# Unit norms behind the next product, the last unit in parts, a rotating third place and statistics by batch in a four-layer convolution kernel

## The chip, the cores and the metric

The kernel runs on one core of one Trainium2 chip, in float32. A core has a matrix engine (TensorE, PE in the profile; its weight loads are PEld), a vector engine (VectorE, DVE), an engine for activation functions (ScalarE, ACT), a general engine (GpSimd, POOL) and one that only starts transfers (SyncE, SP). They run side by side and wait for one another through semaphores. Data come from and go to HBM by DMA; SyncE, ScalarE and GpSimd can start a transfer. The metric is the device time of one execution in microseconds (us), lower is better.

## The reference, cut to what matters

The input x has shape (4, 384, 64, 64). Four layers follow, each of the form `x = x + layer(group_norm(x))`. Layer 0 is an attention block, layer 1 a filter in 8 by 8 Fourier patches with a depthwise convolution, layer 3 a 7 by 7 depthwise convolution with weights made from the data. The change lies in layer 2:

```python
y3 = bn(dw(x, c3_w, 1));  y5 = bn(dw(x, c5_w, 2))        # depthwise 3x3 and 5x5
y1 = x * c1_w + c1_b
tok = bn(kw[:, 0:1] * y3 + kw[:, 1:2] * y5 + y1)
gp = tok.mean(axis=(2, 3));  gh = gelu(bn(pw(gp, cg_w1)))
gates = sigmoid(bn(pw(gh, cg_w2)));  tok = tok * gates
h1 = gelu(bn(pw(tok, cm_w1)))                            # 384 -> 768
h2 = bn(pw(h1, cm_w2))                                   # 768 -> 384
out = gate * (tok + h2) + (1 - gate) * x
```

Each `bn` takes its mean and variance of a channel over all four batches and all positions, so all of a channel's results must exist before the next step can use any.

## The kernel before

**Stages.** Phase A does layers 0 and 1 (0 to 2567 us in the profile). Phase B does the depthwise convolutions of layer 2 and forms tok (2567 to about 3207). Phase EF is the MLP: E multiplies tok by cm_w1 (3207 to 3719), F applies the norm and Gelu and multiplies by cm_w2 (3726 to 4223). Phase G finishes layer 2 and does layer 3 (to the end). The program is written with a tile framework: the code names tiles, buffers and operations, and the framework sets waits and an order on each engine, which follows the order of the code unless an earlier operation isn't ready by its own reckoning; every engine and every DMA queue then runs its list strictly in that order.

**Phase B.** The 384 channels are cut into 12 units of 32. A unit's tile has 128 partitions, which are 4 batches by 32 channels. For a unit u, `unit_strips(u)` loads x1 (tag "x", six buffers, two for each unit), normalises it on ScalarE and, from unit 4 on, transposes it on TensorE (`strip_m`) into the strips tile z; the copies out of PSUM are at L1066 (VectorE) and L1068 (ScalarE). Then 16 steps n follow. In each, `matrices53` builds a band matrix (`toep`, L1114), `conv53` convolves two channels with both kernels (`conv_m`, L1133), ScalarE copies the result (`d_o`, L1142) and VectorE takes its statistics (`st`, L1145); after every fourth step eight channels go to HBM as `d` (L1148). After step 15 `conv_norms(u, st)` makes the scale and shift of the unit's two norms: `cn_rep` (L1164) averages the means, `cn_m` (L1173) sums over batches, a logarithm and an exponential on ScalarE give the inverse root (L312, L313), and L1183 to L1186 end with `s` and `s0`, called cn_s in the trace.

`unit_tok(u)` turns a unit into tok: it loads d back in another layout (`c_d`, L1198), adds x scaled on ScalarE (L1206), 3 by 3 (L1209) and 5 by 5 (L1211) on VectorE, squares on ScalarE (L1216) and writes tok (L1219). It is a generator of eight pieces that run between the convolutions of the next unit: in step n the loop takes a piece of tok for even n and a piece of the next unit's strips for odd n. The last unit has no next one: its eight pieces run after everything, and then `tok_stats` takes the statistics of tok (L1227 and on).

**Phase EF.** E goes through 4 batches b by 4 blocks i of 1024 positions. A tile of tok has three parts of 128 channels: two lie in the tile `e_tok` (two buffers), the third in a part of the strips tile z, at `i % 3 * 1024` (loads at L1342, scaling at L1343). h_s (L1358) is the product, e_h its copy, h_st its statistics (L1367). After the last block six aggregates over all 32 entries of h_st give h_mv (L1385), and `bn_scale_shift` (L312 to L324) the scale and shift for Gelu. F does the same for h2: it takes aggregates by batch (L1426), because the mean by batch is wanted anyway, and over all (L1429).

`over_batches` gives mean and variance over batches from those of each batch; it is used once, for tok ("ar").

Of the kernel before, what the change touches and what calls it, by code (L numbers as in the profile page):

```python
# [21 lines left out]
F32 = mybir.dt.float32  # L22
AF = mybir.ActivationFunctionType
ALU = mybir.AluOpType
AX = mybir.AxisListType
# [201 lines left out]
class _Builder:  # L227
# [99 lines left out]
    def over_batches(self, name, mv):  # L327

        nc = self.nc
        st = self.sm([P, NJ, 6], f"{name}_st")  # L330
        m = self.sm([P, NJ, 2], f"{name}_m")
        for j in range(NJ):
            nc.vector.bn_stats(st[:, j, :], mv[:, j, :, 0])
            nc.vector.bn_aggr(m[:, j, :], st[:, j, :])
        within = self.sm([P, NJ], f"{name}_w")
        nc.vector.tensor_reduce(within, mv[:, :, :, 1], AX.X, ALU.add)
        var = self.sm([P, NJ], f"{name}_v")
        nc.vector.scalar_tensor_tensor(var, within, 1.0 / B, m[:, :, 1], ALU.mult, ALU.add)
        return m[:, :, 0], var

    def bn_of_four(self, name, z, g, b, func, out):

# [620 lines left out]
    def phase_b(self):  # L963

        tc, nc = self.tc, self.nc
        with ExitStack() as ctx:
            self.open_psum(ctx, 2)  # L970
            cp = ctx.enter_context(tc.tile_pool(name="b_const", bufs=1))
            self.bx_p = ctx.enter_context(tc.tile_pool(name="b_x", bufs=6))
            self.bt_p = ctx.enter_context(tc.tile_pool(name="b_t", bufs=2))
            self.bc_p = ctx.enter_context(tc.tile_pool(name="b_c", bufs=3))
            self.band7 = self.const(cp, "band7")
            self.band7_p = self.psum.tile([P, 512], F32, tag="band", name="band7_p", bufs=1)[:, 0:W]
            nc.vector.tensor_copy(self.band7_p, self.band7)
            self.mean128 = cp.tile([P, P], F32, tag="mean128", name="mean128")
            nc.gpsimd.memset(self.mean128, 1.0 / P)
            self.taps53(0)  # L980
            self.toep = {}
            for n in range(4):
                self.matrices53(n)
            for q in range(4):
                x = self.bx_p.tile([P, 2048], F32, tag="x", name="in_x1")[:, 0:1024]
                self.strips5(0, B - 1, x, 8 * q, self.pm)
            self.units(cp)
            self.unit_x = [[] for _ in range(UNITS)]
            for u in range(UNITS):
                st = self.bt_p.tile([P, 2, 16, 6], F32, tag="st", name="st")  # L990
                strips = self.unit_strips(u + 1) if u + 1 < UNITS else iter(())
                tok = self.unit_tok(u - 1) if u else self.unit_strips(0)
                nets = iter(()) if u else self.nets(cp)
                for n in range(16):
                    if u or n > 1:
                        self.matrices53(16 * u + n + 2)
                    self.conv53(u, n, st)
                    next(strips if n % 2 else tok, None)
                    if n % 3 == 2:
                        next(nets, None)  # L1000
                self.conv_norms(u, st)
            for _ in self.unit_tok(UNITS - 1):
                pass
            self.tok_stats()
# [148 lines left out]
    def conv_norms(self, u, st):  # L1153
# [13 lines left out]
        nc.vector.scalar_tensor_tensor(d, parts[:, :, 2], 1.0 / P, d, ALU.mult, ALU.add)  # L1167

        nc.vector.tensor_copy(four[:, 1], spread(d))
        m = self.pm("cn_m")  # L1170
        for k in range(2):
            for v in range(2):
# [12 lines left out]
        nc.vector.scalar_tensor_tensor(s0, m[:, 6:7], -1.0, self.base[:, u : u + 1], ALU.mult, ALU.add)  # L1185
        nc.vector.scalar_tensor_tensor(s0, m[:, 7:8], -1.0, s0, ALU.mult, ALU.add)  # L1186
        self.tok_s = s, s0

    def unit_tok(self, u):

        nc = self.nc
        j, q = u // 4, u % 4
        s, s0 = self.tok_s
        for i in range(4):
            sl = slice(i * 1024, (i + 1) * 1024)
            d5, d3 = (self.bc_p.tile([P, 1024], F32, tag=k, name=f"c_{k}") for k in ("d5", "d3"))
            for v, d in enumerate((d5, d3)):
                nc.sync.dma_start(  # L1198
                    d.rearrange("p (y n) -> p y n", n=P),
                    self.d53[v][u][8 * i : 8 * i + 8].rearrange("y b c n -> (b c) y n"),  # L1200
                )
            for h in range(2):
                part = slice(h * 512, (h + 1) * 512)
                last = u == UNITS - 1
                m = self.psum.tile([P, 512], F32, tag="c" if last else "t", name="tok_m", bufs=4 if last else 1)
                nc.scalar.activation(  # L1206
                    m, self.unit_x[u][i // 2][:, i % 2 * 1024 + h * 512 :][:, 0:512], AF.Identity, bias=s0, scale=self.vec("c1_w")[:, u : u + 1]
                )
                nc.vector.scalar_tensor_tensor(m, d3[:, part], s[:, 1:2], m, ALU.mult, ALU.add)  # L1209
# [72 lines left out]
    def phase_ef(self, strips):  # L1282
        tc, nc = self.tc, self.nc
        with ExitStack() as ctx:
# [45 lines left out]


            st = ep.tile([P, 6, B * 8, 6], F32, tag="h_st", name="h_st")
            sums = cp.tile([P, NJ, B, 4], F32, tag="wx_sum", name="wx_sum")
            for b in range(B):
                for i in range(4):
                    blk = slice(i * 1024, (i + 1) * 1024)
                    t01 = io.tile([P, NJ - 1, 1024], F32, tag="tok", name="e_tok")
                    at = i % 3 * 1024
                    t = [t01[:, 0], t01[:, 1], self.z_[:, at : at + 1024]]
                    for j in range(NJ):  # L1340
                        for q in range(4):
# [53 lines left out]
            for b in range(B):  # L1395
# [415 lines left out]
```

## Time and profile before

| | |
|---|---|
| time, median of three runs | 5031.06 us (5026.48 to 5037.9) |
| profiled execution | span 5034.1 us |
| TensorE busy | 4606.5 us |
| VectorE busy | 2735.1 us |
| ScalarE busy | 2119.4 us |
| phase B, 2567 to 3159 us: TensorE busy | 557.7 of 592 us |
| seam from B to E, 3159 to 3207 us: TensorE busy | 4.9 of 48 us |
| E, 3207 to 3719 us: TensorE busy | 500.4 of 512 us |

A row of the timeline has the start and the time of an instruction or of several that were merged, its engine, its line (L1133 is line 1133 of the kernel before), the operation, out<-in by the program's names, and in brackets how long the engine had been idle and what ended that. SPq is SyncE's list of transfers. A row of the waits view has who waited, for whom, the total in us, the number of waits and the longest. In the waits and timelines "xN" counts records; a float32 matmul leaves two.

### The profile page before, as it was taken

To read this page: it belongs to the slowest core of one execution; us is meant where nothing else is said; L and a number is where in the kernel's file an instruction comes from. 1 tells how busy PE (TensorE), PEld (TensorE's weight loads), DVE (VectorE), ACT (ScalarE), POOL (GpSimd) and SP (SyncE) were. 2 spreads that over 40 slices of the span, in tenths; PEclk is the share of its full clock that TensorE was granted. 3 is DMA by queue.
4 is the path that set the end of the run, shared out by engine and by line. 5 is a ranking of instruction groups with operands and counts; after the bars stand their busy time and mean duration, and the time that the engine had idled before them with its cause. 6 is when DMAs were issued, how large, how long until landed. Compare 5 with 4: busy or idle time off the path is not lost. (4 is left out here: it accounts for less than half of the span.)

```text
span 5034.1 us, 48007 instructions
## 1 busy us (share of the span) xinstructions
PE 4606.5 (92%) x17875; PEld 2617.1 (52%) x17875; DVE 2735.1 (54%) x4480; ACT 2119.4 (42%) x2819; POOL 762.6 (15%) x568
## 2 busy tenths in 40 slices
PE   5999999989999899999989999699999996569999
PEld 2433444334443344435467888344444443559999
DVE  5322456644656445565867778554521114767775
ACT  4444344453544544445345666311133334652320
POOL 1000000000000000000025555000000000135543
PEclk9999999999999999998989999799999997569999
DMA  5110211110111111112259999766664333757876
GB/s 176 61 49 29 90 56 62 57 59 32 69 63 69 42 38 63 63 57 96 93 150 285 290 292 299 257 248 245 244 238 150 150 134 136 255 181 229 235 214 193
DMA packets 344919, 723.30 MB, mean 144 GB/s; under 512 B 22011, under 2 KB 172390, under 8 KB 337766
## 3 DMA queue, kind: packets, MB, share of 16 engines
q1 hardware_dynamic: 283032, 477.56, 30.5%
q0 software_dynamic: 33152, 136.60, 7.2%
q10 hardware_dynamic: 28494, 105.99, 5.4%
q8 instruction: 144, 2.36, 0.2%
q14 instruction: 97, 0.79, 0.0%
HBM read 432.48 MB, written 287.57 MB: 143 GB/s over the span
## 5 line engine op out<-in xcount | busy, mean ns | idle before, releaser
L733 PE MATMUL av<-probs,vt 128*128 128x512 f32 x2048 | 964.2, 606 | 0.0
L704 ACT ACTIVATE probs<-sc_s 128x1024 f32<-128x1024 f32 x512 | 500.1, 1021 | 758.6 <-PE av L733 743.8
L733 PEld LDWEIGHTS av<-probs,vt 128*128 128x128 f32 x2048 | 373.5, 193 | 472.0 <-issue 464.6
L924 DVE SCALAR_TENSOR_TENSOR acc<-band,vecs,acc 128x512 f32<-128x512 f32 x708 | 508.2, 747 | 43.5 <-POOL band L885 25.1
L1133 PE MATMUL conv_m<-toep,z 128*128 128x256 f32 x2304 | 519.0, 385 | 10.6 <-DVE toep L1114 6.4
L1414 PE MATMUL h_m<-f_h,cm_w_t 128*128 128x512 f32 x1152 | 496.2, 594 | 7.9 <-ACT f_h L1401 7.9
L1133 PEld LDWEIGHTS conv_m<-toep,z 128*128 128x128 f32 x2304 | 438.2, 192 | 71.6 <-DVE z L1066 4.9
L1358 PE MATMUL h_s<-e_tok,cm_w_t 128*128 128x512 f32 x768 | 364.5, 598 | 5.5 <-DVE e_tok L1343 5.5
L1414 PEld LDWEIGHTS h_m<-f_h,cm_w_t 128*128 128x128 f32 x1152 | 219.4, 191 | 284.7 <-issue 272.9
L1701 PE MATMUL conv_m<-toep,z 128*128 128x128 f32 x3072 | 367.2, 278 | 0.0
L1114 POOL TENSOR_TENSOR toep<-w,band 128x1536 f32<-128x1536 f32 x94 | 323.8, 3445 | 281.6 <-PE conv_m L1133 248.1
L1701 PEld LDWEIGHTS conv_m<-toep,z 128*128 128x128 f32 x3072 | 358.0, 195 | 0.0
L696 PE MATMUL sc_s<-q,k 32*128 32x512 f32 x2048 | 299.5, 644 | 12.6 <-ACT probs L704 10.9
L847 PE MATMUL t_m<-w_in_t,xb 128*128 128x384 f32 x768 | 278.7, 497 | 1.2 <-DVE k L622 0.6
L766 PE MATMUL proj_m<-xm,w_proj_t 128*128 128x512 f32 x576 | 268.3, 605 | 7.3 <-DVE xm L719 7.3
L1365 ACT COPY e_h<-h_s 128x1024 f32<-128x1024 f32 x96 | 97.2, 1012 | 415.5 <-PE h_s L1358 415.5
L773 DVE SCALAR_TENSOR_TENSOR x_res<-proj_m,bn_c,x_res 128x512 f32<-128x512 f32 x96 | 71.8, 748 | 339.2 <-PE proj_m L766 334.4
L1358 PEld LDWEIGHTS h_s<-e_tok,cm_w_t 128*128 128x128 f32 x768 | 147.6, 192 | 191.4 <-issue 184.6
L1422 DVE BATCH_NORM_STATS2 h_st<-f_h 128x6 f32<-128x512 f32 x72 | 49.8, 694 | 322.9 <-ACT f_h L1421 322.9
L1367 DVE BATCH_NORM_STATS2 h_st<-e_h 128x6 f32<-128x512 f32 x192 | 123.2, 685 | 185.4 <-ACT e_h L1365 185.4
L847 PEld LDWEIGHTS t_m<-w_in_t,xb 128*128 128x128 f32 x768 | 143.8, 192 | 137.1 <-issue 60.3
L1358 PE MATMUL h_s<-z,cm_w_t 128*128 128x512 f32 x384 | 196.8, 595 | 10.5 <-DVE z L1343 10.5
(369 smaller groups left out, 6298.1 us busy)
## 6 DMA issues: line engine op xcount, KB each, us to landing
d<-d_o ACTq DMA_DIRECT2D x96, 512.0 KB
c_d<-d SPq DMA_DIRECT2D x96, 512.0 KB
hid<-e_h ACTq DMA_DIRECT2D x16, 3072.0 KB
f_h<-hid SPq DMA_DIRECT2D x16, 3072.0 KB
x_in<-in_x SPq DMA_DIRECT2D x96, 256.0 KB
x_res<-in_x SPq DMA_DIRECT2D x32, 768.0 KB
xa<-x_res POOLq DMA_DIRECT2D x32, 768.0 KB, 3.7
xa_in<-xa SPq DMA_DIRECT2D x32, 768.0 KB
```

Of the source, the lines that this page charges most:

```text
L696: nc.tensor.matmul(s[:, g], lhsT=k4[32 * g : 32 * g + 32, c], rhs=q[i][32 * g : 32 * g + 32], start=True, stop=True,)
L704: nc.scalar.activation(p[:, h * 1024 : (h + 1) * 1024], s[:, 2 * h : 2 * h + 2].rearrange("p a b -> p (a b)"), AF.Exp, scale=0.25,)
L733: nc.tensor.matmul(av, lhsT=vt[:, 4 * c + v, :], rhs=p[:, v * 512 : (v + 1) * 512], start=c == 0 and v == 0, stop=c == 7 and v == 3,)
L766: nc.tensor.matmul(m, lhsT=self.w_proj[:, j, o * P : (o + 1) * P], rhs=xm[:, j], start=j == 0, stop=j == NJ - 1,)
L847: nc.tensor.matmul(m[:, 0:C], lhsT=xb[:, j], rhs=self.w_in[:, j, :], start=j == 0, stop=j == NJ - 1,)
L924: nc.vector.scalar_tensor_tensor(out, src(j, k), w, done, ALU.mult, ALU.add)
L1114: eng.tensor_tensor(t, self.w53[:, at : at + 192].rearrange("p (m n) -> p m n", n=8).unsqueeze(2).to_broadcast([P, 24, 8, 8]), band.rearra ...
L1133: nc.tensor.matmul(m[:, c * 256 : (c + 1) * 256], lhsT=self.z_[:, at : at + P], rhs=t[:, 12 * c + 4 * i : 12 * c + 4 * i + 4].rearrange("p ...
L1358: nc.tensor.matmul(s[:, v, :], lhsT=w1[:, j, o * P : (o + 1) * P], rhs=t[j][:, v * 512 : (v + 1) * 512], start=j == 0, stop=j == NJ - 1,)
L1367: nc.vector.bn_stats(st[:, o, 8 * b + 2 * i + v, :], h[:, o, v * 512 : (v + 1) * 512])
L1414: nc.tensor.matmul(m, lhsT=w2[:, o, j * P : (j + 1) * P], rhs=h[:, o, v * 512 : (v + 1) * 512], start=o == 0, stop=o == 5,)
L1701: nc.tensor.matmul(m[:, ch * P : (ch + 1) * P], lhsT=self.z_[:, at : at + P], rhs=t[:, 8 * c + 2 * i : 8 * c + 2 * i + 2].rearrange("p m a ...
```

## The change

It has four parts. First, `conv_norms` becomes a generator with two steps, and its steps run after the first and the second convolution of the next unit; a piece of the next unit's strips is now taken for even n, and a piece of tok for odd n, where the scale and shift of the unit before exist. This is to keep TensorE from standing still at the seam of two units. Second, `last_d` loads the last unit's convolution results early and in parts, into four tiles of tag "x" of 2048 columns: after the convolution of step 12 the first half of rows of the 24 channels that are already in HBM; after the loop the second half of those, then the last eight channels, some of them by GpSimd's queue. `unit_tok` of the last unit then reads these tiles. Third, the third part of tok in E goes to the place `(4 * b + i) % 3` rather than `i % 3`. Fourth, the statistics of h and h2 are aggregated for each batch and joined by `over_batches`, which is written anew for any number of columns.

```diff
     def over_batches(self, name, mv):
-        for j in range(NJ):
-            nc.vector.bn_stats(st[:, j, :], mv[:, j, :, 0])
-            nc.vector.bn_aggr(m[:, j, :], st[:, j, :])
-        within = self.sm([P, NJ], f"{name}_w")
-        nc.vector.tensor_reduce(within, mv[:, :, :, 1], AX.X, ALU.add)
-        var = self.sm([P, NJ], f"{name}_v")
-        nc.vector.scalar_tensor_tensor(var, within, 1.0 / B, m[:, :, 1], ALU.mult, ALU.add)
-        return m[:, :, 0], var
+        n = mv.shape[1]
+        mean, var = self.sm([P, n], f"{name}_m"), self.sm([P, n], f"{name}_v")
+        nc.vector.tensor_reduce(mean, mv[:, :, :, 0], AX.X, ALU.add)
+        nc.vector.tensor_scalar(mean, mean, 1.0 / B, None, ALU.mult)
+        d = self.sm([P, n, B], f"{name}_d")
+        nc.vector.tensor_sub(d, mv[:, :, :, 0], mean.unsqueeze(2).to_broadcast([P, n, B]))
+        nc.vector.tensor_mul(d, d, d)
+        nc.vector.tensor_add(d, d, mv[:, :, :, 1])
+        nc.vector.tensor_reduce(var, d, AX.X, ALU.add)
+        nc.vector.tensor_scalar(var, var, 1.0 / B, None, ALU.mult)
+        return mean, var
...
+            norms = iter(())
...
                     self.conv53(u, n, st)
-                    next(strips if n % 2 else tok, None)
+                    next(norms, None)
+                    next(tok if n % 2 else strips, None)
                     if n % 3 == 2:
                         next(nets, None)
-                self.conv_norms(u, st)
+                    if u == UNITS - 1 and n == 12:
+                        self.last_d(0)
+                norms = self.conv_norms(u, st)
+            self.last_d(1)
+            for _ in norms:
+                pass
             for _ in self.unit_tok(UNITS - 1):
                 pass
...
         nc.vector.tensor_copy(four[:, 1], spread(d))
+        yield
         m = self.pm("cn_m")
...
         self.tok_s = s, s0
+        yield
+
+    def last_d(self, step):
+        nc = self.nc
+        if step == 0:
+            self.d_last = {}
+        for h in range(2):
+            if step == h:
+                for v in range(2):
+                    self.d_last[h, v] = self.bx_p.tile([P, 2048], F32, tag="x", name="d_last")
+        parts = [(0, 0)] if step == 0 else [(1, 0), (0, 1), (1, 1)]
+        for h, late in parts:
+            c = slice(24, 32) if late else slice(0, 24)
+            for v in range(2):
+                for b in range(B):
+                    (nc.gpsimd if h and late else nc.sync).dma_start(
+                        self.d_last[h, v][32 * b + c.start : 32 * b + c.stop].rearrange("p (y n) -> p y n", n=P),
+                        self.d53[v][UNITS - 1][16 * h : 16 * h + 16, b, c].rearrange("y c n -> c y n"),
+                    )
...
+            if u == UNITS - 1:
+                d5, d3 = (self.d_last[i // 2, v][:, i % 2 * 1024 :][:, 0:1024] for v in range(2))
+            else:
...
+            hmv = ep.tile([P, 6, B, 2], F32, tag="h_mv", name="h_mv")
...
-                    at = i % 3 * 1024
+                    at = (4 * b + i) % 3 * 1024
...
-            mv = self.sm([P, 6, 2], "h_mv")
-            for o in range(6):
-                nc.vector.bn_aggr(mv[:, o, :], st[:, o].rearrange("p a b -> p (a b)"))
-            a1, c1 = self.bn_scale_shift("bn_h", mv[:, :, 0], mv[:, :, 1], self.vec("cm_g1"), self.vec("cm_b1"))
+                for o in range(6):
+                    nc.vector.bn_aggr(hmv[:, o, b], st[:, o, 8 * b : 8 * b + 8].rearrange("p a b -> p (a b)"))
+            a1, c1 = self.bn_scale_shift("bn_h", *self.over_batches("h", hmv), self.vec("cm_g1"), self.vec("cm_b1"))
...
-            mv = self.sm([P, NJ, 2], "h2_mv")
-            for j in range(NJ):
-                nc.vector.bn_aggr(mv[:, j, :], st2[:, j].rearrange("p a b -> p (a b)"))
-            a2, c2 = self.bn_scale_shift("bn_h2", mv[:, :, 0], mv[:, :, 1], self.vec("cm_g2"), self.vec("cm_b2"))
+            a2, c2 = self.bn_scale_shift("bn_h2", *self.over_batches("h2", mvb), self.vec("cm_g2"), self.vec("cm_b2"))
```

More of the change, by code (lines that the diff above doesn't have):

```diff
@@ L329, in over_batches @@
         nc = self.nc
-        st = self.sm([P, NJ, 6], f"{name}_st")
-        m = self.sm([P, NJ, 2], f"{name}_m")
-        for j in range(NJ):
-            nc.vector.bn_stats(st[:, j, :], mv[:, j, :, 0])
-            nc.vector.bn_aggr(m[:, j, :], st[:, j, :])
-        within = self.sm([P, NJ], f"{name}_w")
-        nc.vector.tensor_reduce(within, mv[:, :, :, 1], AX.X, ALU.add)
-        var = self.sm([P, NJ], f"{name}_v")
-        nc.vector.scalar_tensor_tensor(var, within, 1.0 / B, m[:, :, 1], ALU.mult, ALU.add)
-        return m[:, :, 0], var
+        n = mv.shape[1]
[9 more added lines that the diff above has]
+        return mean, var
     def bn_of_four(self, name, z, g, b, func, out):
@@ L1195, in unit_tok @@
             sl = slice(i * 1024, (i + 1) * 1024)
[L1196 to L1201, printed above, removed]
+            if u == UNITS - 1:
+                d5, d3 = (self.d_last[i // 2, v][:, i % 2 * 1024 :][:, 0:1024] for v in range(2))
+            else:
+                d5, d3 = (self.bc_p.tile([P, 1024], F32, tag=k, name=f"c_{k}") for k in ("d5", "d3"))
+                for v, d in enumerate((d5, d3)):
+                    nc.sync.dma_start(
+                        d.rearrange("p (y n) -> p y n", n=P),
+                        self.d53[v][u][8 * i : 8 * i + 8].rearrange("y b c n -> (b c) y n"),
+                    )
             for h in range(2):
```

## The prediction

> **What bounds the kernel now.** I read the page first (the 40 slices and the busy times), then sums by stage (the windows view), then the waits of TensorE and the timeline around each place that the diff touches. One page line sets the frame:
>
> ```profile
> PE 4606.5 (92%) x17875; PEld 2617.1 (52%) x17875; DVE 2735.1 (54%) x4480; ACT 2119.4 (42%) x2819; POOL 762.6 (15%) x568
> ```
>
> TensorE is busy for 92% of the span, so time can only come from its pauses. The windows view says where some lie (columns: window, its length, then busy us of PE, PEld, DVE, ACT, POOL, granted clock, DMA share, GB/s):
>
> ```profile
> 2871.00:2919.00 48.00, 46.59 (x234) 40.76 (x234) 38.38 (x74) 30.69 (x48) 27.38 (x9) 1.00 0.99 295
> 3159.00:3207.00 48.00, 4.91 (x22) 4.15 (x22) 20.00 (x76) 27.01 (x40) 0.00 (x0) 0.50 0.91 280
> 3207.00:3719.00 512.00, 500.39 (x1152) 220.38 (x1152) 258.56 (x390) 96.77 (x96) 11.47 (x16) 0.99 0.64 238
> ```
>
> The first row is one of the twelve units of phase B: TensorE rests 1.4 of 48 us, but the DMA share is 0.99. The second is the seam from B to the first MLP product, where TensorE does almost nothing for 48 us. The third is that product, 512 us with some 12 us of rest. The seam between two units, in the timeline:
>
> ```profile
> 2868.92 1.15 PE L1061 MATMUL strip_m<-ident,unit_x 128*128 128x128 f32 x8 [0.24 <-ACT z L1068]
> 2870.56 1.05 DVE L1066 COPY z<-strip_m 128x512 f32<-128x512 f32 x1
> 2870.79 0.42 PE L1164 MATMUL cn_rep<-st,mean 128*128 128x64 f32 x2 [0.72 <-DVE st L1145]
> 2871.67 1.99 PE L1133 MATMUL conv_m<-toep,z 128*128 128x256 f32 x8 [0.45 <-DVE z L1066]
> ```
>
> The norms' first product (cn_rep) stands on TensorE ahead of the next unit's first convolution and waits for the statistics of the last one; then the convolution waits for the copy of the last strip. The end of phase B:
>
> ```profile
> 3161.41 10.95 SPq L1198 DMA_DIRECT2D c_d<-d  x6
> 3163.63 0.16 DVE L1186 SCALAR_TENSOR_TENSOR cn_s<-cn_m,cn_s 128x1 f32<-128x1 f32 x1
> 3172.70 1.41 DVE L1209 SCALAR_TENSOR_TENSOR tok_m<-c_d,cn_s,tok_m 128x512 f32<-128x512 f32 x2 [8.91 <-DMA c_d<-d]
> 3187.39 0.25 DVE L1227 TENSOR_REDUCE tok_mv<-tok_sum 128x12 f32<-128x96 f32 x1
> ```
>
> The scale and shift are ready at 3163.8, but the convolution results of the last unit come back from HBM only at 3172.7. And the MLP product at the turn from batch 0 to batch 1, first in the waits of TensorE, then VectorE's and then TensorE's timeline:
>
> ```profile
> PE h_s L1358 <- DVE z L1343: 10.5, 3, 4.2
> ```
>
> ```profile
> 3338.83 0.81 DVE L1343 TENSOR_SCALAR z<-z,at,ct 128x1024 f32<-128x1024 f32 x1 [3.64 <-DMA z<-tok]
> ```
>
> ```profile
> 3339.70 1.56 PE L1358 MATMUL h_s<-z,cm_w_t 128*128 128x512 f32 x2 [3.44 <-DVE z L1343]
> 3341.05 3.19 PE L1358 MATMUL h_s<-e_tok,cm_w_t 128*128 128x512 f32 x4
> ```
>
> Three waits, one at each turn of the batch: the third place of tok goes 0, 1, 2, 0 and then 0 again, so the load has to wait for the tile before. The four matmuls after it take 3.19 us, where four take 1.7 elsewhere.
>
> [...] matmul records start 0.43 us apart in this product and 0.85 apart, four times, after the first two waits (3.4 and 4.2 us); after the third (2.9 us) none is slow. [...] the trace has 1.28 us, twice in each unit's norms (logarithm, exponential), so from cn_m to the shift takes some 5 us whatever the order.
>
> **Part 1, norms behind the next product; strips one convolution earlier.** In units 5 to 10 the cn_rep products start 48.2 us apart. The pauses at each seam (0.24, 0.72, 0.45 us and some short ones; 48.0 less 46.6 busy) are 1.4 us. After the change the next unit's first convolution (12 records of 0.214 us, 2.6 us) stands before cn_rep, and the statistics need about 1.85 us after the last convolution (the wait of cn_rep at 2619.70); the last strip is copied one convolution earlier. Both waits should be covered: 7 seams by 1.4 = 9.8, and 1.7 for a stretch at half clock after one of them (unit 8 takes 49.9 us). The first four seams are worse. Start to start on TensorE, less normal spacing: 1.65 + 2.6 and 2.1 of half clock (seam at 2619.7), 3.35 + 1.3 (2674.0), 1.65 + 1.35 (2719.3), 1.6 + 1.7 (2772.7): 17.3. But here ScalarE and the DMAs are behind for other reasons (a pause of 3.4 us before a convolution at 2696.9 that has nothing to do with norms), so I count a little over half, 9.5. Sum 21; lower end 5 (see the rivals), upper 28.8. New waits: tok's pieces and the scale and shift come one convolution later. Behind them on ScalarE and VectorE stand the copies and statistics of the next convolutions, which have four PSUM buffers, some 10 us of slack, so I charge nothing.
>
> **Part 2, last unit in parts.** The bytes stay (4 MB), the eight loads become 32. Eight go out at n = 12, under the last three convolutions (DMA share 0.86 there), eight more without the last eight channels when the slot of the unit before is free, at about 3157. The last channels are written at 3157.65 and seen as landed at 3161.4. Their first eight loads then cost 8 x 0.41 us of issue on SyncE (mean of c_d<-d) = 3.3, so 3164.7 at the earliest, and 3166 with the transfer. By bandwidth: 1.05 MB of writes, 1.57 MB and 0.52 MB of loads from 3157.65 at 280 GB/s end at 3168.9. I take 3168; the upper end is 3172.7, no gain. The shift may be 2.5 us late, since tok's last piece of unit 10 now comes after the last convolution: 3166, still earlier. From there VectorE needs four pieces of 2.66 us (3172.70 to 3175.36) = 10.7, so 3178.7 in place of 3187.4: 8.6; I take 8 (0 to 11). The chain behind it, to the first MLP matmul at 3207.4, is serial work of VectorE, ScalarE and TensorE and moves with it.
>
> **Part 3, the third place rotates.** (4b + i) % 3 never gives the same place to two tiles in a row; a place is now free two tiles (of 31 us) ahead. Removed: 10.5 us of waits and twice four matmuls at 0.43 extra = 3.4: 14. What could take its place is the load of the other two thirds (e_tok, two buffers), but at the other turns of i, where these alone bind, TensorE does not wait. 12 to 15.
>
> **Part 4, statistics by batch.** over_batches becomes seven dependent small VectorE operations; such ones start 0.2 us apart (3187.67, 3187.88, 3188.09), so 1.4 us. For ar the logarithm starts at 3192.32, after a table load that hides the old chain; the new one ends at 3192.65: +0.35. For h the last aggregate of 192 elements (1.02) becomes one of 48 (0.29 to the next start) plus 1.4: +0.7. For h2 0.96 becomes 1.4: +0.45. Together +1.5 on the path (0.5 to 2.5). The 24 aggregates by batch (0.37 each, 8.9 us instead of 6.1) lie in a stage where VectorE is busy for 259 of 512 us: nothing.
>
> **Sum.** 21 + 8 + 14 - 1.5 = 41.5; 5031.1 - 41.5 = 4989.6, say 4990.
>
> **Rivals.**
> A, the DMAs become the bound of phase B. For it: share 0.97 to 0.99 in units 4 to 10 at 292 GB/s. Against it: these units last 48.20 to 48.21 us each, with the same pauses at the same places, so TensorE's order sets them; and the first MLP product moves 315 GB/s in one stretch (3240 to 3300). If so, part 1 gives only 5, part 2 4: 5 + 4 + 14 - 1.5 = 21.5, time 5009.5.
> B, the tail gives nothing: the last write waits for the early loads of the same tensor, or 24 issues on one queue cost what they save. Time 4998.
> C, slower: tok's later turn frees the input slots later, loads of the next strips come 2.6 us late in each unit[...]: 11 x 4.3 = 47 lost, tail 0, 14 won, 1.5 lost: 5031 + 34.5 = 5065.5. Against it: six input buffers for three units.
>
> **How the numbers follow.** Chances: forecast 0.58, A 0.24, B 0.11, C 0.07. Range: all upper ends of the parts (28.8 + 11 + 15 - 0.5 = 54.3) give 4977, and A with another 3 us lost gives 5013; I put 4975 to 5013, which leaves out C and some of the tails. Faster by over 0.2% (below 5021): the first three cases less a small share, 0.88; same 0.05; slower 0.07.
>
> **What would show it.** Right: units 5 to 10 take 46.8 us with no wait at cn_rep; VectorE's first piece of the last unit starts near 3168 less what was gained before; no TensorE wait for z in the first product, which takes 497 us; the aggregate chains longer by half a us each. Wrong: units still at 48.2 us with waits on DMA (A), the write d<-d_o late (B), waits of strips or of ScalarE for x (C).

## The result, and the profile after

The changed kernel takes 5084.59 us (median of four runs, 5080.53 to 5093.9); the kernel before took 5034.48 beside it (5026.48 to 5045.41). The ratio is 1.0101, with a 95% interval of 1.0076 to 1.0125: slower by 1%, where 4990 us was forecast. The profiled execution is 47.3 us longer (span 5081.4), and the page says that TensorE works only 7.9 us more of it (4606.5 us busy before), so the rest are pauses:

```profile
PE 4614.4 (91%) x17875; PEld 2623.6 (52%) x17875; DVE 2733.3 (54%) x4508; ACT 2120.9 (42%) x2819; POOL 767.0 (15%) x576
```

The table cuts the profiled executions at events of the trace: B is from the first to the last copy `d_o` of a convolution, the seam from there to the first `h_s` matmul, E from the first to the last `h_s`, each from start to start. What lies before B (2560 to 2574 us) and after F (798 to 807) scatters by these amounts over all runs, without a change of code there, so that the three stages tell more than a single time.

| us | before | after | difference | predicted |
|---|---|---|---|---|
| B | 586.2 | 619.4 | +33.2 | -21 (part 1) |
| seam | 50.4 | 76.5 | +26.1 | -8 (part 2), +0.35 (part 4) |
| E | 510.3 | 496.9 | -13.4 | -14 (part 3) |
| last h_s to first product of F | 8.48 | 9.32 | +0.84 | +0.7 (part 4) |
| last product of F to the next | 7.66 | 8.21 | +0.55 | +0.45 (part 4) |

So parts 3 and 4 did what was worked out, and parts 1 and 2 did the opposite. The windows view of the changed kernel has the same three stretches as were shown before (window, length, busy us of PE, PEld, DVE, ACT, POOL, granted clock, DMA share, GB/s): a unit of phase B, the seam, and E.

```profile
2884.52:2935.78 51.26, 46.52 (x237) 40.66 (x235) 37.69 (x71) 29.92 (x48) 27.47 (x8) 1.00 0.86 268
3187.00:3263.00 76.00, 5.29 (x24) 4.46 (x24) 24.21 (x83) 28.83 (x43) 4.82 (x8) 0.52 0.83 188
3263.00:3760.00 497.00, 496.62 (x1151) 219.85 (x1152) 258.99 (x405) 96.19 (x95) 11.54 (x16) 0.99 0.65 242
```

In the unit TensorE now rests 4.7 us in place of 1.4, yet the DMA share has fallen from 0.99 to 0.86: the transfers aren't the bound, they are asked for too late. In E the rest is gone (0.4 of 497 us).

**Phase B.** The waits view of units 4 to 10 of the changed kernel, for TensorE, VectorE and GpSimd (total us, times, longest):

```profile
PE conv_m L1142 <- DVE z L1075: 25.4, 7, 5.2
...
DVE tok_m L1243 <- DMA c_d<-d: 38.9, 7, 6.9
...
POOL toep L1123 <- DMA w<-in_c_t: 55.7, 8, 8.4
```

The same view of the kernel before has, for its units 4 to 10:

```profile
PE conv_m L1133 <- DVE z L1066: 3.2, 7, 0.5
...
DVE tok_m L1209 <- DMA c_d<-d: 4.9, 5, 2.0
```

The wait for `cn_rep` that the change was to remove is in fact gone, and unit 1 falls from 46.7 to 42.2 us. But the convolution at each seam now waits for the strip copy `z`: 25.4 us where it was 3.2 before. In the same units VectorE waits 38.9 us for `c_d`, before 4.9. Nearly all of the loss lies in these units: from the first copy of unit 4 to that of unit 11 it is 371.3 us in place of 339.2, while units 1 to 3 together take as long as before. How the two hang together shows at one seam, first in SyncE's list and then on VectorE and TensorE (timeline of the changed kernel):

```profile
2908.23 0.34 SPq L1253 DMA_DIRECT2D tok<-c_d  x1
2908.62 1.65 SPq L1056 DMA_DIRECT2D unit_x<-x  x2
2916.53 0.34 SPq L1253 DMA_DIRECT2D tok<-c_d  x1
2916.98 1.44 SPq L1232 DMA_DIRECT2D c_d<-d  x2
2918.53 1.40 SPq L1109 DMA_DIRECT2D w<-in_c_t  x1
2920.35 3.71 SPq L1232 DMA_DIRECT2D c_d<-d  x2
```

```profile
2924.20 0.76 DVE L1243 SCALAR_TENSOR_TENSOR tok_m<-c_d,cn_s,tok_m 128x512 f32<-128x512 f32 x1 [4.45 <-DMA c_d<-d]
...
2925.97 1.04 PE L1070 MATMUL strip_m<-ident,unit_x 128*128 128x128 f32 x8
...
2931.69 1.07 DVE L1075 COPY z<-strip_m 128x512 f32<-128x512 f32 x1
...
2932.91 2.83 PE L1142 MATMUL conv_m<-toep,z 128*128 128x256 f32 x12 [3.74 <-DVE z L1075]
```

SyncE issues two loads of x, then stands 6.3 us before a write of tok that waits for VectorE's piece. Only then, at 2916.98, does it reach the loads of `c_d` and `w` for the next pieces. VectorE runs its own list in order as well: it stands 4.45 us before the tok piece, and the copy of the strip, whose transposes are done at 2927.0, comes up at 2931.69. TensorE waits for that copy. A late load has become a late convolution by way of a piece of work that TensorE itself doesn't need.

The kernel before has loads of `c_d` behind a waiting write of tok as well (SyncE's list, then VectorE):

```profile
2909.08 0.34 SPq L1219 DMA_DIRECT2D tok<-c_d  x1
2909.51 1.48 SPq L1198 DMA_DIRECT2D c_d<-d  x2
```

```profile
2919.65 0.76 DVE L1209 SCALAR_TENSOR_TENSOR tok_m<-c_d,cn_s,tok_m 128x512 f32<-128x512 f32 x1
```

There the piece that reads them comes 10.1 us after their issue and doesn't wait. In the changed kernel VectorE is ready for its piece at 2919.75, 2.8 us after the issue.

**The tail.** SyncE's list and VectorE's first piece of the last unit, in the changed kernel's timeline:

```profile
3181.96 13.26 SPq L1215 DMA_DIRECT2D d_last<-d  x7
3195.32 0.37 SPq L1253 DMA_DIRECT2D tok<-c_d  x1
3206.35 17.09 SPq L1215 DMA_DIRECT2D d_last<-d  x16
...
3232.11 1.41 DVE L1243 SCALAR_TENSOR_TENSOR tok_m<-d_last,cn_s,tok_m 128x512 f32<-128x512 f32 x2 [34.42 <-DMA e_tok<-tok]
```

The last copy of a convolution ends phase B at 3186.9; the first piece starts 45 us later, before it was 15.7 (3157.0 to 3172.70). The row names a load of `e_tok`, which came last by the records; what the piece reads is `d_last`. The last sixteen loads start one every 1.07 us (17.09 / 16), where 0.41 had been counted; 7.0 us of this are recorded as waits, 3.8 for another weight and 3.2 for earlier ones of these loads. Before the sixteen, SyncE stands for another reason (its waits view, 3176 to 3240):

```profile
SPq L1215 <- DMA cm_w_t<-in_cm_w_t: 10.6, 1, 10.6
```

This is the transfer of a weight that ScalarE has issued at 3195.09.

**E and the statistics.** In E only the wait at its start is left among TensorE's waits, and the logarithm of "ar" waits 0.31 us for the new chain (waits and timeline of the changed kernel):

```profile
PE h_s L1393 <- DVE e_tok L1378: 5.7, 1, 5.7
```

```profile
3247.87 0.17 DVE L339 TENSOR_SCALAR ar_v<-ar_v 128x3 f32<-128x3 f32 x1
3248.07 0.30 ACT L312 ACTIVATE bn_ar_a<-ar_v,eps 128x3 f32<-128x3 f32 x1 [0.31 <-DVE ar_v L339]
```

### The profile page after: what moved, and what is told of

It reads as the page before. It is cut to its first block, busy times and chain, and to the rows that moved or that the text cites. A ratio compares the mean times of both kernels' runs of the same rounds, so it can differ in the third digit from the quotient of the medians.

```text
span 5081.4 us, 48036 instructions
## 1 busy us (share of the span) xinstructions
PE 4614.4 (91%) x17875; PEld 2623.6 (52%) x17875; DVE 2733.3 (54%) x4508; ACT 2120.9 (42%) x2819; POOL 767.0 (15%) x576
## 5 line engine op out<-in xcount | busy, mean ns | idle before, releaser
L1142 PE MATMUL conv_m<-toep,z 128*128 128x256 f32 x2304 | 533.7, 391 | 35.8 <-DVE z L1075 29.1
L1448 PE MATMUL h_m<-f_h,cm_w_t 128*128 128x512 f32 x1152 | 497.0, 594 | 8.7 <-ACT f_h L1435 8.7
L697 PE MATMUL sc_s<-q,k 32*128 32x512 f32 x2048 | 298.9, 643 | 13.4 <-ACT probs L705 10.9
```

Source lines behind the costliest of these rows:

```text
L697: nc.tensor.matmul(s[:, g], lhsT=k4[32 * g : 32 * g + 32, c], rhs=q[i][32 * g : 32 * g + 32], start=True, stop=True,)
L1142: nc.tensor.matmul(m[:, c * 256 : (c + 1) * 256], lhsT=self.z_[:, at : at + P], rhs=t[:, 12 * c + 4 * i : 12 * c + 4 * i + 4].rearrange("p ...
L1448: nc.tensor.matmul(m, lhsT=w2[:, o, j * P : (j + 1) * P], rhs=h[:, o, v * 512 : (v + 1) * 512], start=o == 0, stop=o == 5,)
```

## The experiments

All are edits of the kernel before, each beside runs of it on the same chip. The stages are those of the table above.

| run | time, us | ratio to before (95%) | B | seam | E |
|---|---|---|---|---|---|
| rotation alone | 5008.07 | 0.9954 (0.9937 to 0.9971) | 587.4 | 50.0 | 495.9 |
| loop alone (part 1) | 5068.63 | 1.0083 (1.0056 to 1.0110) | 623.3 | 51.1 | 512.3 |
| last unit in parts alone (part 2) | 5058.97 | 1.0055 (1.0038 to 1.0073) | 586.3 | 76.4 | 511.6 |
| turns swapped alone | 5060.40 | 1.0047 (1.0030 to 1.0063) | 613.3 | 51.7 | 513.3 |
| norms deferred alone | 5031.74 | 0.9988 (0.9978 to 0.9998) | 578.9 | 52.9 | 514.5 |
| loop, tok written by GpSimd | 5027.34 | 0.9988 (0.9978 to 0.9998) | 575.8 | 52.3 | 512.1 |
| last loads cut by batch | 5054.32 | 1.0035 (1.0025 to 1.0046) | 587.9 | 66.9 | 514.7 |
| last loads cut by rows | 5038.35 | 1.0007 (0.9997 to 1.0017) | 586.0 | 50.7 | 512.6 |
| in parts, a weight on another queue | 5058.56 | 1.0040 (1.0025 to 1.0054) | 585.8 | 74.5 | 513.7 |
| four whole loads | 5036.00 | 1.0004 (0.9995 to 1.0013) | 585.7 | 50.3 | 509.1 |
| 16 loads by batch | 5041.85 | 1.0014 (1.0003 to 1.0024) | 586.2 | 57.3 | 513.8 |
| 16 loads by rows | 5033.76 | 0.9999 (0.9989 to 1.0009) | 587.6 | 48.6 | 511.4 |
| first combination | 5016.31 | 0.9966 (0.9954 to 0.9978) | 575.5 | 57.2 | 495.8 |
| second combination | 5011.77 | 0.9955 (0.9941 to 0.9969) | 576.5 | 51.0 | 497.0 |

### Each part alone

```diff
-                    at = i % 3 * 1024
+                    at = (4 * b + i) % 3 * 1024
```

> The kernel before with part 3 alone. Theory: the rotating place removes the three z waits and the half clock behind two of them, and nothing else moves: 13 to 15 us faster than before (5020 if before is 5034), no wait of TensorE for z in the first MLP product, which takes 497 us from first to last start. Rival: the gain only appeared in the changed kernel because its other stages moved: 0 to 5 us.

E falls by 14.4 us, to 495.9. (The half clock shows in the kernel before as a granted clock of 0.50 from 3340.30 to 3343.70 and from 3470.00 to 3473.40, behind the waits of 3.4 and 4.2 us; behind the third, from 3597.90 to 3601.30, it is 1.00.) Part 3 holds alone as in the whole: E is 495.8 to 497.0 in the four kernels with the rotation and 509.1 to 514.7 in the others. The time fell by more, 26.7 us; most of the rest lies before B and after F (9.7 and 6.3 us in the profiled executions), where no code differs.

The loop alone is part 1 as in the change (`conv_norms` in two steps, and):

```diff
-                    next(strips if n % 2 else tok, None)
+                    next(norms, None)
+                    next(tok if n % 2 else strips, None)
```

> The kernel before with part 1 alone (norms in two steps behind the next products, tok and strips swapped between even and odd steps); loads of the last unit, third place and statistics as before. Theory: the loss inside phase B is made here: units 4 to 10 take 50 to 55 us instead of 48.2, phase B's convolutions end some 30 us later, and the run is 25 to 35 us slower than before. Rival: the early loads of the last unit or the changed SBUF use cause it; then this run is within 10 us of before or faster.

B grows by 37.1 us and nothing else moves: the loss in phase B is part 1's own.

The last unit in parts alone is `last_d` of the change, with `last_d(0)` after step 12 and `last_d(1)` after the last norms:

```diff
+                    if u == UNITS - 1 and n == 12:
+                        self.last_d(0)
                 self.conv_norms(u, st)
+            self.last_d(1)
```

> The kernel before with part 2 alone (the last unit's results in 32 loads). Theory: the tail loss is made here by the number and shape of the loads: the time from the last convolution to the first MLP product grows from 50.4 to 70 to 80 us, units are as before, run 20 to 30 us slower. Rival: the tail only suffers because part 1 leaves a backlog of transfers and of tok pieces; then this run is as before or up to 9 us faster.

The seam is 76.4 us without anything of part 1: the second loss is part 2's own. The three differences by ratio, -0.46, +0.83 and +0.55%, add up to 0.92% of the whole's 1.01%. Part 4 was not run alone; what is said of it comes from the changed kernel's trace.

### What in the loop costs: the swap of turns, not the deferred norms

The swap alone, the norms left where they were:

```diff
-                    next(strips if n % 2 else tok, None)
+                    next(tok if n % 2 else strips, None)
```

> The kernel before with only the swap: tok's pieces in odd steps, strips in even ones; conv_norms stays where it was. Theory: the order in SyncE's list follows from the swap (both writes of tok stand ahead of the next loads), so this alone makes most of part 1's loss: 15 to 35 us slower, with waits of VectorE for c_d and of GpSimd for w. Rival: the later norms make the loss; then this is within 8 us of before.

B is 613.3, which is 27.1 us of the loop's 37.1, and units 4 to 10 show the signature of the changed kernel (waits view of this run):

```profile
PE conv_m L1133 <- DVE z L1066: 21.4, 7, 3.9
...
DVE tok_m L1209 <- DMA c_d<-d: 29.6, 14, 5.0
```

The deferral alone keeps the strips on odd steps:

```diff
-                    next(strips if n % 2 else tok, None)
+                    next(norms, None)
+                    if n % 2 or (u and n == 0):
+                        next(strips if n % 2 else iter(()), None)
+                    else:
+                        next(tok, None)
+                    if u and n == 15:
+                        next(tok, None)
...
-                self.conv_norms(u, st)
+                norms = self.conv_norms(u, st)
```

> The norms alone are put behind the next unit's products, in two steps; the strips keep their odd convolutions and tok's pieces the even ones (from the third on, the eighth after the last). Theory 1 (it is the swap of turns that costs, through the order of SyncE's list; the deferred norms are harmless): phase B is not longer than before, 575 to 588 us, time 5020 to 5036. Theory 2 (the deferral itself costs, because the scale and shift and so all of tok's pieces come later): phase B 600 us or more, time 5048 or more.

B falls to 578.9: theory 1. So the deferral alone is harmless and pays a little, in units 2 and 3 (49.2 to 43.3 and 54.6 to 49.6 us). On top of the swap it costs another 10 us (613.3 to 623.3); why was not followed up. But units 4 to 10 mostly stay at 48.2, and the timeline of TensorE shows why:

```profile
2896.60 1.15 PE L1070 MATMUL strip_m<-ident,unit_x 128*128 128x128 f32 x8 [0.24 <-ACT z L1077]
2898.46 0.43 PE L1173 MATMUL cn_rep<-st,mean 128*128 128x64 f32 x2 [0.72 <-DVE st L1154]
2899.34 5.45 PE L1142 MATMUL conv_m<-toep,z 128*128 128x256 f32 x24 [0.46 <-DVE z L1075]
```

Although the code has the norms after the first convolution, the framework's list has `cn_rep` ahead of it, presumably because the convolution has to wait for the last strip. The 0.72, 0.24 and 0.46 us of the kernel before are all still there. In units 4 to 10 of the kernels with the swap and tok's writes on SyncE (turns swapped, loop alone, the whole change) no wait at `cn_rep` is recorded; the longer wait for `z` stands in its place.

### Why the swap costs: loads behind writes in one list

This is the loop alone, with one line more changed in `unit_tok`:

```diff
-            nc.sync.dma_start(self.tok[u, :, :, sl].rearrange("b c n -> (b c) n"), d5)
+            nc.gpsimd.dma_start(self.tok[u, :, :, sl].rearrange("b c n -> (b c) n"), d5)
```

> The loop of the change alone (norms deferred, turns swapped), with the writes of tok issued by GpSimd in place of SyncE. Theory 1 (the loads of c_d and w stand in SyncE's list behind writes of tok that wait for VectorE): the waits of VectorE for c_d and of GpSimd for w fall to a few us in all, phase B falls from 623 to 586 or less, time 5035 or less. Theory 2 (the loads are late for another reason[...]): phase B stays at 610 to 625, time 5060 to 5070. A write on GpSimd that waits for VectorE could hold up GpSimd's own products (toep): then PE's waits for toep grow.

B falls from 623.3 to 575.8 us by the queue of one transfer alone. In units 4 to 10 (waits view of this run):

```profile
PE cn_rep L1168 <- DVE st L1149: 7.1, 5, 2.3
PE conv_m L1137 <- DVE z L1070: 6.0, 7, 1.8
...
DVE tok_m L1215 <- DMA c_d<-d: 2.9, 2, 1.8
...
POOL tok L1225 <- DVE c_d L1217: 30.9, 13, 4.6
```

The write's wait for VectorE has moved to GpSimd's list, where it holds up nothing that TensorE waits for (no wait for `toep` shows), and the waits for `c_d` are nearly gone. Over five kernels the waits of units 4 to 10 line up with B:

| us | DVE for c_d | PE for z | GpSimd for w | B |
|---|---|---|---|---|
| loop alone | 32.9 | 24.8 | 53.4 | 623.3 |
| turns swapped | 29.6 | 21.4 | 72.8 | 613.3 |
| before | 4.9 | 3.2 | 1.8 | 586.2 |
| norms deferred | 0 | 3.0 | 69.2 | 578.9 |
| loop, tok by GpSimd | 2.9 | 6.0 | 0 | 575.8 |

GpSimd's wait for `w` doesn't go with B (69.2 us where B is short): it is the late `c_d`, through VectorE's list, that costs. Nor is it SyncE's standing as such: before writes of tok it stands some 130 us in units 4 to 10 of the kernel before, 180 in the changed one, and in the run with the norms deferred (its waits view)

```profile
SPq L1230 <- DVE c_d L1222: 167.8, 28, 8.1
```

though no `c_d` is late there. The standing costs where the loads behind the write are needed soon after it, as in the seam above. That the swap brings this about is shown by the run with the turns swapped; how it moves VectorE's pieces closer to the writes was not worked out.

### Why the last unit's loads are slow

With the parts alone, SyncE's rows at the tail are

```profile
3145.20 9.26 SPq L1207 DMA_DIRECT2D d_last<-d  x8
3160.55 0.35 SPq L1245 DMA_DIRECT2D tok<-c_d  x1
3161.01 26.29 SPq L1207 DMA_DIRECT2D d_last<-d  x16
```

and SyncE was recorded as waiting 8.5 us for the transfer of a weight. To the parts alone, this run adds that the transfer of one weight, `cm_w2_t`, is given to another queue:

```diff
-            w2 = self.weight(cp, "cm_w2_t")
+            w2 = cp.tile(list(self.ins["cm_w2_t"].shape), F32, tag="cm_w2_t", name="cm_w2_t")
+            nc.gpsimd.dma_start(w2, self.ins["cm_w2_t"])
```

> The last unit's results in parts, alone (seam 76.4 us, time 5059), with the load of the weights cm_w2_t, which fell into the same stretch on ScalarE's queue, issued by GpSimd. Theory 1 (the first part loads wait 8 to 10 us[...]): the seam shortens by 8 to 10, to 66 to 68, time 5050. Theory 2 (the wait only hides the transfer, which is slow in itself): seam within 3 us of 76.

The seam is 74.5 in place of 76.4, and the last 16 loads take as long as before (26.31 us of issue):

```profile
3166.00 26.31 SPq L1207 DMA_DIRECT2D d_last<-d  x16
```

But the run doesn't decide between the theories (the loads wait for a weight, or are slow in themselves), because the edit moved the wrong weight. The views leave numbers out of names, and two weights are called `cm_w_t`. The one that SyncE waits for is `cm_w1_t`; ScalarE still issues it here, and the wait is as long as it was (ScalarE's timeline and SyncE's waits of this run):

```profile
3165.58 0.34 ACTq L282 DMA_DIRECT2D cm_w_t<-in_cm_w_t  x1
```

```profile
SPq L1207 <- DMA cm_w_t<-in_cm_w_t: 8.6, 1, 8.6
```

The one that was moved goes out only at 3215.42, after all of the loads. So no run tests whether the weight holds up the loads, and the 8.5 us (10.6 in the changed kernel) stay open. Next, number against width: the kernel before, with each of the last unit's loads in `unit_tok` replaced, at the same place, by

```diff
+                    for b in range(B):
+                        nc.sync.dma_start(
+                            d[32 * b : 32 * b + 32].rearrange("p (y n) -> p y n", n=P),
+                            self.d53[v][u][8 * i : 8 * i + 8, b].rearrange("y c n -> c y n"),
+                        )
```

> The kernel before, with each of the eight loads of the last unit's results cut into four, one for each batch (32 partitions of 8 rows), at the same place in the list. The seam from the last copy of convolution results to the first MLP product is 50.4 us before and 76.5 after. Theory 1 (32 loads on one queue cost issue time[...]): seam 60 us or more. Theory 2 (it is the narrow loads of 24 and 8 partitions, in pieces of 512 bytes, that are slow): seam 50 to 54, time within 5 us of the kernel before.

The seam is 66.9, and by the letter of the expectation that spoke for the number of loads. The same number cut the other way contradicts it:

```diff
+                    for y in range(0, 8, 2):
+                        nc.sync.dma_start(
+                            d[:, P * y : P * y + 2 * P].rearrange("p (y n) -> p y n", n=P),
+                            self.d53[v][u][8 * i + y : 8 * i + y + 2].rearrange("y b c n -> (b c) y n"),
+                        )
```

> As the run with each of the last unit's eight loads cut into four by batch (32 partitions of 8 rows, seam 66.9 us), but cut by rows: all 128 partitions and 2 rows each. Number, bytes and place of the 32 loads are the same. Theory 1 (narrow loads are slow because they reach few partitions at a time): seam 50 to 55, and the 512-byte packets take some 0.027 us at the median, as they do in whole loads, where the loads of 32 partitions took 0.040. Theory 2 (32 loads are slow for their number, issue and completion): seam 63 or more.

The seam is 50.7: 32 loads cost nothing if each reaches all partitions. But the pair isn't quite clean: by batch, SyncE's list has the first write of tok after 11 loads, by rows after 18. So the loads were put into the four input slots, where no write stands among them. `last_d` is called once, after the last norms. First it loads whole:

```diff
+                nc.sync.dma_start(
+                    d.rearrange("p (y n) -> p y n", n=P),
+                    self.d53[v][UNITS - 1][16 * h : 16 * h + 16].rearrange("y b c n -> (b c) y n"),
+                )
```

> The last unit's results loaded into the four input slots as in the change, but in four loads of all 128 partitions and 16 rows each, put out after the last write; no part is loaded early. The seam is 50.4 us before and 76.4 with the parts alone. Theory 1 (what costs is the narrowness and the number of the part loads, not the slots or the place): seam 44 to 52 us, time 5025 to 5036. Theory 2 (the input slots come free late, or the other loads that now stand ahead hold it up): seam 60 us or more, time 5045 or more.

The seam is 50.3, as before the change: the slots and the place in the list cost nothing, and bring nothing either. Then a matched pair, 16 loads of equal bytes at this place, cut by batch (32 partitions) and by rows (128). By batch:

```diff
+                for b in range(B):
+                    nc.sync.dma_start(
+                        d[32 * b : 32 * b + 32].rearrange("p (y n) -> p y n", n=P),
+                        self.d53[v][UNITS - 1][16 * h : 16 * h + 16, b].rearrange("y c n -> c y n"),
+                    )
```

> The last unit's results into the four input slots after the last write, as in the run with four whole loads (seam 50.3 us), but each load cut into four by batch: 16 loads of 32 partitions and 16 rows. No write of tok stands among them. If narrow loads are slow in themselves: packets of 512 bytes at 0.035 us or more, the 16 loads take 18 us or more from the first issue to the last landing's reader, seam 54 to 62. If the long seam of the loads cut by batch before (66.9) was only the order of the list, with writes of tok among the loads: seam 50 to 52.

By rows:

```diff
+                for y in range(0, 16, 4):
+                    nc.sync.dma_start(
+                        d[:, P * y : P * y + 4 * P].rearrange("p (y n) -> p y n", n=P),
+                        self.d53[v][UNITS - 1][16 * h + y : 16 * h + y + 4].rearrange("y b c n -> (b c) y n"),
+                    )
```

> The pair of the run above: the same 16 loads in number and bytes, cut by rows: 128 partitions and 4 rows each. If narrowness is what costs: packets at 0.027 to 0.030 us, seam 49 to 52. If 16 loads in place of four cost by their number: seam as in the run above.

Seams of 57.3 and 48.6: with number, bytes and place equal, 32 partitions cost 8.7 us against 128. (SyncE's record has 3.5 us of waiting for the weight by batch, and none by rows.) The windows view in the midst of the loads, for the loads by batch, then by rows, and last the changed kernel (24 and 8 partitions); the last two columns are the DMA share and GB/s:

```profile
3166.00:3180.00 14.00, 0.00 (x0) 0.00 (x0) 4.74 (x11) 2.61 (x4) 0.00 (x0) 0.50 1.22 193
```

```profile
3170.00:3182.00 12.00, 0.00 (x0) 0.00 (x0) 5.49 (x12) 4.33 (x6) 0.00 (x0) 0.50 1.13 297
```

```profile
3208.00:3222.00 14.00, 0.00 (x0) 0.00 (x0) 0.00 (x0) 0.00 (x0) 0.00 (x0) 0.50 0.90 122
```

297 GB/s with 128 partitions, 193 with 32, 122 with 24 and 8, all queues together, at a DMA share of 0.9 and more in each (the sum of the packets' times over that of 16 engines; the 1.22 stand for 19.5 packets under way on average). SyncE's queue alone moves 256, 187 and 119 GB/s in these stretches, and in the trace's packet records those of 512 bytes on it take 0.032, 0.051 and 0.052 us at the median. So in the loads with 32 partitions the packets took longer (0.051 against 0.032); in those with 24 and 8 about as long as with 32, but fewer were under way at a time: the packets of SyncE's queue fill 102% of 16 engines' time with 128 partitions, 119 with 32 and 84 with 24 and 8. Why a packet takes longer in a load of few partitions was not shown. The changed kernel's own stretches, the wait for the weight and then the last sixteen loads, are

```profile
3196.00:3206.00 10.00, 0.00 (x0) 0.00 (x0) 0.64 (x4) 3.79 (x6) 2.98 (x6) 0.50 1.04 222
3206.00:3232.00 26.00, 0.00 (x0) 0.00 (x0) 0.00 (x0) 0.00 (x0) 0.00 (x0) 0.50 0.83 104
```

The 2.7 MB of the second stretch (26 us at 104 GB/s) would take about 10 us at the forecast's 280 GB/s. So, as an estimate from these two rates, slow loads make some 16 of the 26 us that the seam grew; the other 10 lie about the wait, during which 222 GB/s still went through. It isn't a proof: the first eight loads run in part before the seam.

### Putting together what paid

The first combination takes the loop with tok's writes on GpSimd, the rotation, and the four whole loads for the last unit:

```diff
-                    next(strips if n % 2 else tok, None)
+                    next(norms, None)
+                    next(tok if n % 2 else strips, None)
...
-            nc.sync.dma_start(self.tok[u, :, :, sl].rearrange("b c n -> (b c) n"), d5)
+            nc.gpsimd.dma_start(self.tok[u, :, :, sl].rearrange("b c n -> (b c) n"), d5)
...
-                    at = i % 3 * 1024
+                    at = (4 * b + i) % 3 * 1024
...
+            self.last_d(1)
```

> A version meant to keep what paid: tok's third place rotates (-14 us measured alone), norms deferred and turns swapped with the writes of tok on GpSimd's queue (phase B 575.8 us in place of 586), the last unit's results in four whole loads; the statistics as before. If the gains add up: E stage 496 us, phase B 576, seam 45 to 52, time 5003 to 5012 (the kernel before at 5034). If the tail's loads collide with writes of tok on GpSimd, the seam is 55 or more and the time 5015 or more.

B and E come as expected, but the seam is 57.2. The statistics of tok start 30.4 us after the last copy, as before; what follows is late, as ScalarE shows (timeline of this run):

```profile
3184.74 1.28 ACT L312 ACT_TABLE_LOAD   x1 [9.25 <-DMA tok<-d_last]
```

Ahead of the logarithm ScalarE issues a weight load (at 3184.36), and the row puts 9.25 us of waiting down to a write of tok; the same place had 2.35 us before. (The table load itself is the one of 1.28 us that the forecast counts twice in each unit's norms.) What in the order of the transfers made it so was not tried. The second combination is the first with the last unit's loads as in the kernel before:

```diff
-            self.last_d(1)
```

> The loop of the change with the writes of tok on GpSimd, and the rotating third place; the last unit's loads and the statistics as in the kernel before. The two were measured apart: phase B 575.8 us with a seam of 52.3, and 14 us less in the first MLP product. If they add up, phase B is 576, the seam 52, the product 496, and the time 5034 - 10 + 2 - 14 = 5012 (0.9953 to 0.9960 of the kernel before). If the writes on GpSimd's queue disturb the product or the seam when the places rotate, 5018 or more.

5011.77 us: B 576.5, seam 51.0, E 497.0. It and the rotation alone (5008.07) are the fastest; their intervals overlap, so which of them is better stays open, though B is 10.9 us shorter in this one.

## Why the prediction was wrong

**Part 1: the step that failed is "New waits".** It named what stands behind tok's pieces on ScalarE and VectorE, the copies and statistics of the next convolutions with some 10 us of slack, and charged nothing. It missed two lists. On SyncE, the loads of the next pieces stand behind writes of tok that wait for VectorE. On VectorE, the copy of the next strip, for which the next convolution waits directly, stands behind the piece that waits for its load. The cost was +33 in place of -21. Rival C had the sign and the swap as the cause, but not the mechanism: it had the input slots come free late (47 us). Its 4.3 us for each unit are the 2.6 by which loads come late and 1.7 for slow matmuls; such do show (granted clock 0.96 from 2764 to 3139 in the changed kernel, 0.99 from 2764 to 3109 before), but TensorE's busy time there is only 4.0 us longer (339.12 against 335.12). Loads late by the order of the list, with the slots untouched, explain it, since moving the write alone brings B to 575.8. Nor does SyncE wait for slots: in units 4 to 10 of the changed kernel no load of x is recorded as waiting for a piece of tok, the last reader of its slot. In the run with tok's writes on GpSimd such waits come to 42.4 us, and B is short.

The gain lay elsewhere than worked out. With the write out of the way B is 10.4 us shorter, where 21 had been counted. Units 0 to 3 are 15.6 us shorter; the forecast had 9.5 for their four seams. Units 4 to 10, where the other 11.5 was to come from, are together 4.5 us longer (343.7 against 339.2): the waits for `cn_rep` and `z` are 7.1 and 6.0 us there, before 5.0 and 3.2. The 46.8 us for units 5 to 10 were never reached throughout (46.5 to 54.0 in the second combination), and with the norms deferred alone the list kept `cn_rep` in front.

**Part 2: the term that failed is "at 280 GB/s".** That rate comes from whole loads of 128 partitions; the part loads reach 24 and 8 and ran at 104 to 122 GB/s. The issue cost of 0.41 us per load was also from whole loads; here a load started every 1.07 us, waits included. (Even the whole loads of the tail, in the forecast's own row, are six in 10.95 us.) The start was late as well: the second eight were to go out at the end of the last convolution, but SyncE's last sixteen began at 3206.35, 19.5 us after its copy, with 10.6 us of a recorded wait for a weight that the forecast hadn't. How much of the loss belongs to that wait stays open. The input slots cost nothing (seam 50.3 with four whole loads), and from the first piece on the tail went as worked out: the statistics of tok start 10.7 us later. Rival B, "the tail gives nothing", wasn't bad enough.

**Part 3** was right: -13.4 in the whole and -14.4 alone, against -14. The waits (10.5 us) are gone, and with them the slow matmuls (0.85 us from start to start): from 3276 to 3760 in the changed kernel TensorE is busy for 484 of 484 us, at a granted clock of 1.00.

**Part 4** was right: +0.31, +0.84 and +0.55 us, sum 1.7, against 1.5. In the fourteen other kernels the wait before F is 8.47 or 8.48 us, as before the change, and in the changed one 9.32.

**Rival A**, the DMAs as the bound of phase B, is out: its share fell to 0.86 in the slow units, and B went to 575.8 with the same bytes. (Its units were not all equal: the one from 2923.22 took 49.9 us.)

## What to carry to other kernels

Before work is moved in a loop, write down the list of each queue in its new order, transfers included, and ask of each waiting entry what stands behind it: a store that waits for a compute engine should not stand in the same list ahead of loads that this engine needs soon (to move it brought B from 623.3 to 575.8 us here). When a transfer is cut to start it earlier, cut it so that every part still reaches all 128 partitions; a part that reaches a quarter of them ran at two thirds of the rate here (193 against 297 GB/s), and parts of 24 and 8 at two fifths (122). And price a part load by a row of its own shape, not by the row of the whole.

## What the runs showed of the hardware that was not expected

- A DMA share near 1 didn't mean a full rate: the share was 0.90 at 122 GB/s and 1.13 at 297, with mostly packets of 512 bytes in both. The share has to be read together with GB/s.
- Not separated by any run: why the loads of 24 partitions and of 8 have fewer packets under way than those of 32 (84 against 119% of 16 engines' time), how much of the changed kernel's seam comes from the loads of eight partitions on GpSimd's queue, and how much from SyncE's wait for the weight.
